# Cross-attention and a mixture of experts on one core: block products over halves of whole experts, and TensorE turning the rows of the first two experts

## The chip, the cores and the metric

The kernel runs on one core of a Trainium2 chip. The metric is the device time of one execution in microseconds (us); the times shown are the median of three runs. The core's engines work side by side, each through its own queue in order: TensorE (PE) multiplies matrices, VectorE (DVE) and ScalarE (ACT) work on elements, GpSimd (POOL) issues the indirect DMAs, and SyncE (SP) issues the plain DMAs. They wait for each other on semaphores.

## The reference

There are 2048 tokens (16 batches of 128) of 512 features. A cross-attention with 32 query heads and 8 key heads of 16 features is added to them; then a feed-forward layer of experts is added:

```python
x = x + xattn(layernorm(x), ctx, ctx)
h = layernorm(x).reshape(-1, 512)
tidx, tw = gate(h)                      # 8 of 32 experts for each token
g = einsum('td,eid->tei', h, w1)        # 512 -> 256 for each expert
u = einsum('td,eid->tei', h, w3)
a = silu(g) * u
routed = einsum('tei,edi,te->td', a, w2, comb)   # comb holds tw at tidx, else 0
out = x + routed + (silu(h @ sw1.T) * (h @ sw3.T)) @ sw2.T
```

All of it is in f32. Only the experts that the gate chose for a token count, so an expert has 2048 x 8 / 32 = 512 tokens on average.

## The kernel before

Attention, the shared expert and the gate come first. What the change touches is the stage of the 32 experts, from about 213 us to the end. The kernel sorts the tokens by expert into 138 slices of 128 slots. The experts stand in a fixed order of places (`ORDER`), each with a fixed capacity (`CAPS`, a multiple of 32) and a room for its tokens (`ROOM`, 440 to 704). A slice that lies on the border of two experts holds rows of both. `begins[k]` is the first slot of place k.

**Rows.** GpSimd gathers each slice's rows by an indirect DMA into one of eight buffers (`gather`, L1432). The rows must be turned, so that the features stand on partitions. For the first slices TensorE does it (`turn`, L1456: sixteen small transposes for two slices, which ScalarE copies out of PSUM, L1473). For all others VectorE transposes blocks of 32x32 inside the slice (`transpose`, L1515, into `blocks`), and ScalarE, with some help from VectorE, copies quarters of 32 tokens into place (`block_copies`, L1512): four copies for each quarter, one for each group of 32 features. Copies for slices that lie next to each other are merged into one. `weigh` (L1524) picks each slot's weight; only then may the buffer be gathered into again.

**Pieces.** The rows of an expert are cut into pieces of at most 512, in buffers `xnT` (four of them) with the results of the up products in `acts` (four). An expert with a capacity over 512, and the first and the last, has two pieces, cut at a multiple of 128 slots; others have one. For an expert of 660 rows the pieces have 384 and 276.

**Up products.** For the first and the last expert they are plain (`direct`, `up`, L1546). For the other thirty they are done by seven block products instead of eight (`seven`, L1615): w1 and w3 (256x512 each, both handled at once in one PSUM bank, the columns of w1 in its first half and those of w3 in its second) are cut into 2x2 blocks, and so are the rows, along the features and along the tokens. VectorE forms sums of weight blocks once per expert (`weight_sums`, L1579: s1, s2, s3, s4, of which s3 overwrites a weight block), sums of token blocks once per piece (`token_sums`, L1610: t1 to t4), and adds the products up (L1643). Each product is four matmuls of 128x128 weights by half a piece's columns. The first product is copied out of PSUM by ScalarE (L1657) before the fifth adds to the same bank; a bank is used twice for three of the four banks of a piece. Silu is ScalarE's (L1651), its product with the other half VectorE's (L1652).

**Down products.** `down` (L1723) multiplies 128 slots by w2 of their expert or experts, two matmuls of 512 columns; ScalarE scales the result by the slots' weights (L1739), and GpSimd adds the rows into the output in HBM (`send`, L1695). Sends of one expert wait for those of the expert before.

**Order.** The order of the work is written out by hand. The loop at the end goes over the pieces, seven steps each (four for `direct`). At each step it issues one product on TensorE, then what became due by it (`soon`, `tick`), then a share of the side work for VectorE and ScalarE (`on_DVE`, `on_ACT`: sums of weights and tokens for the next piece, transposes three pieces ahead, copies two pieces ahead), spread evenly over the steps, then down products of the piece before as planned. One finished slice is always held back (`KEPT`). Weights are loaded three experts ahead, w1 and w3 after an expert's last product, w2 after its last down product (`load_weights`, L1088).

Of the kernel before, what the change touches and what calls it, by code (L numbers as in the profile page):

```python
# [18 lines left out]
P = 128  # L19
# [27 lines left out]
def tile_xattn_moe(  # L47
# [38 lines left out]
    xs = [xpool.tile([P, D], F32, tag=f"x{b}", name=f"x{b}") for b in range(B)]  # L86
    xnT = [
        xtp.tile([P, ND, TB], F32, tag=f"xnT{k}", name=f"xnT{k}") for k in range(NTB)
# [59 lines left out]
    fp = ctx.enter_context(tc.tile_pool(name="fp", bufs=2))  # L148
# [102 lines left out]
    acts = [sap.tile([P, NI, TB], F32, name=f"sa{k}") for k in range(NTB)]  # L251
# [774 lines left out]
    def experts(ups, in_order, later, products):  # L1026
# [384 lines left out]
        for k in range(E):  # L1411
            first, end = begins[k], begins[k + 1]
            if end - first > TB or k in (0, E - 1):
                middle = (first + end + P) // 2 // P * P
                pieces += [(k, first, middle), (k, middle, end)]
            else:
                pieces.append((k, first, end))

        def parts(j):

            for n, (k, first, end) in enumerate(pieces):
                a, b = max(first, j * P), min(end, (j + 1) * P)
                if a < b:
                    yield n, a - j * P, b - j * P, a - first

# [42 lines left out]
        def turned(j, tr, copy):  # L1468
            for n, a, b, col in parts(j):
                for h in range(2):  # L1470
                    a0, b0 = max(a, h * H), min(b, (h + 1) * H)
                    if a0 < b0:
                        copy(  # L1473
                            xnT[n % NTB][:, :, col + a0 - a : col + b0 - a],
# [6 lines left out]
        def block_copies(js):  # L1481
# [3 lines left out]
            for q in range(4):  # L1485
                for j in js:
                    for n, a, b, col in parts(j):
                        if a <= q * Q < b:
                            r, to = j % NB_BUF, col - a
                            last = runs[-1] if runs else None  # L1490
                            if (
                                last
                                and last[0] == q
                                and last[1] == n
                                and last[2] + last[4] == r
                                and last[3] + last[4] * P == to
                            ):
                                last[4] += 1
                            else:
                                runs.append([q, n, r, to, 1])  # L1500
            for q, n, r, to, many in runs:
                for c in range(4):
                    of = blocks[q * Q : (q + 1) * Q, r : r + many, :]
                    of = of.rearrange("p s (k c j) -> p s k c j", c=4, j=Q)[:, :, :, c, :]
                    dst = xnT[n % NTB][c * Q : (c + 1) * Q]
                    at = min(max(to, 0), TB - many * P)
                    dst = dst[:, :, at : at + many * P]
                    dst = dst.rearrange("p k (s t) -> p s k t", t=P)
                    dst = dst[:, :, :, to + q * Q - at : to + (q + 1) * Q - at]
# [8 lines left out]
        def weigh(j):  # L1518
            t = xg.pop(j)
            weighed.add(j)  # L1520
            ks = [pieces[n][0] for n, *_ in parts(j)]
# [17 lines left out]
        def up(n, i, w, banks):  # L1539

            k, first, end = pieces[n]
            m = min(end, begins[k] + ROOM[ORDER[k]]) - first

            acc = banks[w] = ps_p.tile([P, TB], F32, tag="p", name="gu")
            for d in range(ND):
# [3 lines left out]
                    rhs=xnT[n % NTB][:, d, 0:m],  # L1549
# [7 lines left out]
            else:  # L1557
# [3 lines left out]
                        acts[n % NTB][:, i, 0:m], sl[:, 0:m], acc[:, 0:m], ALU.mult  # L1561
# [26 lines left out]
        def width(n):  # L1588
            k, first, end = pieces[n]
            return min(end, begins[k] + ROOM[ORDER[k]]) - first  # L1590

        def halves_of(n):
            h = width(n) // 2
            t = xnT[n % NTB]
            return [t[:, d : d + 2, c * h : (c + 1) * h] for d in (0, 2) for c in range(2)]
# [3 lines left out]
        def token_sums(n):  # L1599


            h = width(n) // 2
            b11, b12, b21, b22 = halves_of(n)
            t1, t2, t4 = (
                late.tile([P, 2, M], F32, tag=name, name=name)[:, :, 0:h]
                for name in ("t1", "t2", "t4")
            )
            tsums[n] = t1, t2, b12, t4
# [3 lines left out]
        def product(acc, w, x, h, first=True):  # L1612
            for i in range(2):
                for d in range(2):
# [5 lines left out]
                        stop=(i == d == 1),  # L1620
# [3 lines left out]
        def seven(n):  # L1624


            k = pieces[n][0]
            h = width(n) // 2
# [4 lines left out]
            b11, _, b21, b22 = halves_of(n)  # L1633
            t1, t2, t3, t4 = tsums.pop(n)

            def bank():
                return ps_p.tile([P, 2, M], F32, tag="p", name="p")

            def kept(name, bufs=2):
                return late.tile([P, 2, M], F32, tag=name, name=name, bufs=bufs)[:, :, 0:h]  # L1640

            def add(out_, a, b):
                soon(lambda: nc.vector.tensor_tensor(out_, a, b, ALU.add))  # L1643

            def gated(of, to, after):
                sl = late.tile([P, 2, M], F32, tag="sg", name="sg", bufs=3)
                if len(of.shape) == 4:
                    sl, g, u = sl[:, :, 0:h], of[:, :, 0], of[:, :, 1]
                else:
                    sl, g, u = sl[:, 0, 0:h], of[:, 0], of[:, 1]  # L1650
                soon(lambda: nc.scalar.activation(sl, g, AF.Silu), after)  # L1651
                soon(lambda: nc.vector.tensor_tensor(to, sl, u, ALU.mult), after + 1)  # L1652

            act = acts[n % NTB]
# [143 lines left out]
        for n in range(len(pieces)):  # L1798
# [41 lines left out]
            for step, _ in enumerate(seven(n) if fast(k) else direct(n)):  # L1840
                tick()
                done += dues[step]
                if step == 1 and by_PE:
                    turn(by_PE)
# [104 lines left out]
```

## Time and profile before

| | us |
|---|---|
| median of three runs | 896.81 (896.02 to 899.05) |
| the profiled execution | 894.69 |
| its span | 892.9 |
| TensorE busy | 872.7 |
| ScalarE busy | 640.9 |
| VectorE busy | 639.3 |
| GpSimd busy | 505.4 |
| first rows of experts turned on TensorE (L1456) | 213.5 |
| last matmul | ends near 883.4 |

Busy times are those of instructions on the engine; those of matmuls overlap, so that two of them can be busy at once. "Idle" times name what ended them. PE stands for TensorE's matmuls, PEld for its weight loads, which run beside matmuls; each f32 matmul of the program shows as two records of each. The granted clock is TensorE's, as a share of full speed.

### The profile page before, as it was taken

What the parts mean: (1) busy time and instruction counts of PE and PEld (TensorE: products, weight loads), DVE (VectorE), ACT (ScalarE), POOL (GpSimd) and SP (SyncE); (2) the same over time, 40 slices, a digit from 0 to 9 for tenths busy, and PEclk for the clock granted to TensorE, in tenths of its full rate; (3) what the DMA queues carried; (4) which work ended last, traced back from release to release, by engine and by line L of the source; (5) the groups of instructions that cost most, each with busy time, mean ns of one, the idle gap of its engine ahead of it and who ended that gap; (6) DMA issues with size and microseconds to landing.
All of it is one profiled execution on the core that took longest, in us unless ns stands there. A gap on an engine that the chain in (4) does not pass through costs nothing.

```text
span 892.9 us, 15745 instructions
## 1 busy us (share of the span) xinstructions
PE 872.7 (98%) x5055; PEld 608.4 (68%) x5055; DVE 639.3 (72%) x1739; ACT 640.9 (72%) x1338; POOL 505.4 (57%) x622
## 2 busy tenths in 40 slices
PE   9999999998999999999999999999999999999995
PEld 5344444544777877878787878787877777777773
DVE  7877778884778776767786777777897767776510
ACT  5888722331989868777888887888897777787441
POOL 4486652674556546556565665666666665543444
PEclk9999999999999999999999999999999999999998
DMA  9111113416578786778787878787877887666534
GB/s 320 40 48 49 48 48 114 145 62 213 161 146 196 159 205 156 175 161 197 175 201 174 208 175 188 179 181 182 203 189 184 195 224 192 156 135 163 81 66 55
DMA packets 59884, 137.28 MB, mean 154 GB/s; under 512 B 12168, under 2 KB 16392, under 8 KB 59792
## 3 DMA queue, kind: packets, MB, share of 16 engines
q0 software_dynamic: 32032, 69.25, 40.4%
q1 hardware_dynamic: 27680, 66.81, 21.9%
q8 instruction: 42, 0.69, 0.4%
q14 instruction: 50, 0.41, 0.2%
q10 hardware_dynamic: 80, 0.13, 0.1%
HBM read 96.71 MB, written 46.73 MB: 161 GB/s over the span
## 4 chain that ended last, share of the span: by engine, by line
PE 93%; issue 2%; POOL 1%; ACT 1%; DVE 1%; DMA 1%; POOLq 0%; ACTq 0%; DVEq 0%
PE p L1615 44%; PE y L1723 25%; PE gu L260 6%; PE sc L465 5%; PE oT L481 3%; PE y L1348 3%; PE x L435 2%; PE gu L1546 2%; POOL out_dram L1695 1%; PE tok L1012 1%; DMA out_dram<-yw,token 1%; PE warm L331 1%; PE lgT L542 0%; PE lg L557 0%; ACT p L475 0%
## 5 line engine op out<-in xcount | busy, mean ns | idle before, releaser
L1695 POOL DMA_INDIRECT out_dram<-yw,token x150 | 244.3, 1629 | 223.6 <-ACT yw L1739 157.5
L1512 ACT COPY xnT<-blocks 32x256 f32<-32x256 f32 (+3 forms) x843 | 358.6, 425 | 11.8
L1723 PE MATMUL y<-wdn,sa 128*128 128x512 f32 (+2 forms) x672 | 259.5, 594 | 0.0
L1615 PE MATMUL p<-xnT,wup 128*128 128x192 f32 (+26 forms) x1152 | 189.6, 311 | 1.2 <-ACT p L1657 1.2
L1615 PEld LDWEIGHTS p<-xnT,wup 128*128 128x128 f32 x1152 | 170.3, 191 | 24.3 <-issue 16.2
L1432 POOL DMA_INDIRECT xgs<-rows,token x138 | 146.8, 1063 | 70.3 <-issue 25.4
L1739 ACT ACTIVATE yw<-y,wt 128x512 f32<-128x512 f32 x138 | 94.8, 687 | 105.5 <-PE y L1723 61.4
L1723 PEld LDWEIGHTS y<-wdn,sa 128*128 128x128 f32 (+2 forms) x672 | 96.1, 171 | 72.8 <-issue 70.0
L1615 PEld LDWEIGHTS p<-t,s 128*128 128x128 f32 x768 | 116.6, 191 | 25.3 <-issue 22.7
L1615 PE MATMUL p<-t,s 128*128 128x128 f32 (+26 forms) x768 | 126.5, 310 | 0.0
L1515 DVE STREAM_TRANSPOSE blocks<-xgs 128x512 f32<-128x512 f32 x134 | 94.8, 707 | 2.9 <-DMA out_dram<-x 2.4
L1643 DVE TENSOR_TENSOR z<-u,p 128x256 f32<-128x256 f32 (+26 forms) x96 | 48.6, 506 | 41.7 <-PE p L1615 38.0
L1615 PEld LDWEIGHTS p<-t,wup 128*128 128x128 f32 x384 | 59.4, 190 | 19.4 <-issue 14.4
L475 ACT ACTIVATE p<-sc 128x1024 f32<-128x1024 f32 x64 | 62.1, 1024 | 13.5 <-PE sc L465 13.5
L1643 DVE TENSOR_TENSOR u<-u,p 128x256 f32<-128x256 f32 (+26 forms) x48 | 24.4, 509 | 58.0 <-PE p L1615 53.3
L1615 PE MATMUL p<-xnT,s 128*128 128x128 f32 (+26 forms) x384 | 64.3, 310 | 0.0
L1615 PE MATMUL p<-t,wup 128*128 128x128 f32 (+26 forms) x384 | 64.0, 310 | 0.0
L1615 PEld LDWEIGHTS p<-xnT,s 128*128 128x128 f32 x384 | 57.2, 191 | 6.1 <-issue 4.5
L260 PE MATMUL gu<-xnT,sup 128*128 128x512 f32 x128 | 59.0, 601 | 0.7 <-ACT ssl L268 0.7
L1006 POOL TENSOR_SCALAR hq<-slice_q,sq 128x138 f16<-128x138 f16 x32 | 35.2, 1113 | 36.3 <-DVE sq L1314 20.1
L1610 DVE TENSOR_TENSOR t<-xnT,t 128x256 f32<-128x256 f32 (+26 forms) x96 | 48.9, 510 | 0.9
L465 PE MATMUL sc<-qT,kz 32*128 32x512 f32 x256 | 44.2, 639 | 0.5 <-DVE qT L456 0.2
(216 smaller groups left out, 1007.4 us busy)
## 6 DMA issues: line engine op xcount, KB each, us to landing
wup<-in_w_dram SPq DMA_DIRECT2D x64, 512.0 KB
wdn<-in_w_dram SPq DMA_DIRECT2D x32, 512.0 KB
rows<-xn SPq DMA_DIRECT2D x16, 256.0 KB
out_dram<-x SPq DMA_DIRECT2D x16, 256.0 KB
x<-in_x_dram SPq DMA_DIRECT2D x15, 256.0 KB
out_dram<-yw,token POOLq DMA_INDIRECT x150
xgs<-rows,token POOLq DMA_INDIRECT x138
cTs<-in_cT_dram SPq DMA_DIRECT2D x4, 256.0 KB
```

The lines of the kernel that those rows point to most:

```text
L260: nc.tensor.matmul(acc, lhsT=sup[:, w, d, ts(i, P)], rhs=xnT[k][:, d, :], start=(d == 0), stop=(d == ND - 1),)
L465: nc.tensor.matmul(scs[j // 2][:, j % 2], lhsT=kzs[b // 4 % 2][rows, b % 4, i, :], rhs=qT[rows], start=True, stop=True, tile_position=(j * ...
L475: nc.scalar.activation(p, sc, AF.Exp, scale=1.0 / HD**0.5)
L1432: nc.gpsimd.indirect_dma_start(out=t, out_offset=None, in_=rows[:, :], in_offset=bass.IndirectOffsetOnAxis(ap=token[:, j : j + 1], axis=0) ...
L1512: yield on_ACT, 1 + many, lambda dst=dst, of=of, copy=copy: copy(dst, of)
L1515: nc.vector.transpose(blocks[:, j % NB_BUF, :], xgs[:, j % NG_BUF, 0:D])
L1610: yield lambda o=out_, a=a, b=b: nc.vector.tensor_tensor(o, a, b, ALU.subtract)
L1615: nc.tensor.matmul(acc[:, i, 0:h], lhsT=w[:, i, d, :], rhs=x[:, d, :], start=(first and i == d == 0), stop=(i == d == 1), skip_group_check ...
L1643: soon(lambda: nc.vector.tensor_tensor(out_, a, b, ALU.add))
L1695: ins = nc.gpsimd.indirect_dma_start(out=flat, out_offset=bass.IndirectOffsetOnAxis(ap=token2[:, k - 1 : k] if a else token[0:b, j : j + 1 ...
L1723: nc.tensor.matmul(y[c0:c1, :], lhsT=acts[n % NTB][:, i, col : col + c1 - c0], rhs=wdn[pieces[n][0] % NW][:, i, :], start=(i == 0), stop=( ...
L1739: nc.scalar.activation(yws[j], y, AF.Copy, scale=wt[:, j : j + 1])
```

## The change

- Every expert now has two pieces. Those of the thirty experts with block products are cut at half the room (`ROOM[ORDER[k]] // 2`), wherever that falls in a slice, and the halves are the token blocks of the seven products: there is one set of seven products for the whole expert.
- An expert with room for up to 512 rows does w1 and w3 together in a bank as before (`both`). A larger one has more columns than half a bank: it does the seven products for w1, then the seven for w3, each of two matmuls per product, in banks of their own. Silu then stands in `act` itself until the w3 pass multiplies it.
- Buffers: one tile `xall` holds the old `xnT` and five half buffers (`half`, 384 columns), another the results of three whole experts (`acts_of`). `blocks` has nine slices and not ten; two finished slices are held back and not one.
- Copies out of the blocks follow the pieces: where a piece begins or ends inside a quarter of 32 tokens, only the tokens of that piece are copied, by a copy of their own. Transposes are now four (half) pieces ahead, copies three.
- TensorE turns all slices of the first two experts (ten), two at a time after each step of the first expert's two pieces; before, it turned four.
- Sums of the next expert's weights are formed in the first half of an expert, sums of its tokens in the second. Down products of the expert before are spread over both halves.

The core of the diff:

```diff
+    HM = max(CAPS) // 2
+    HW = 3 * P
+    NH = 5
+    NA = 3
+    aall = sap.tile([P, NA * NI * 2 * HM], F32, name="sa")
...
+    half = [
+        xall[:, r * ND * HW : (r + 1) * ND * HW].rearrange("p (d t) -> p d t", d=ND)
+        for r in range(NH)
+    ]
...
-            if end - first > TB or k in (0, E - 1):
+            middle = first + ROOM[ORDER[k]] // 2
+            if k in (0, E - 1):
                 middle = (first + end + P) // 2 // P * P
-                pieces += [(k, first, middle), (k, middle, end)]
-            else:
-                pieces.append((k, first, end))
+            pieces += [(k, first, middle), (k, middle, end)]
...
+                    lo, hi = max(a, q * Q), min(b, (q + 1) * Q)
+                    if lo >= hi:
+                        continue
+                    r, to = j % NB_BUF, col + lo - a
+                    last = runs[-1] if runs and runs[-1][0] == q else None
+                    if (
+                        hi - lo == Q
+                        and last
+                        and last[4] == Q
+                        and last[1] + last[5] == r
+                        and last[3] + last[5] * P == to
+                    ):
+                        last[5] += 1
+                    else:
+                        runs.append([q, r, lo - q * Q, to, hi - lo, 1])
...
-        def product(acc, w, x, h, first=True):
-            for i in range(2):
+        def product(acc, w, x, first=True):
+            h = x.shape[-1]
+            outs = range(w.shape[1])
+            for i in outs:
                 for d in range(2):
                     nc.tensor.matmul(
                         acc[:, i, 0:h],
                         lhsT=w[:, i, d, :],
                         rhs=x[:, d, :],
...
-        def seven(n):
+        def seven(k):
+            h = ROOM[ORDER[k]] // 2
+            act = acts_of[k % NA]
...
+            both = 2 * h <= TB
+            size = M if both else HM
...
+            for w in (slice(0, 2),) if both else (slice(0, 1), slice(1, 2)):
+                many = w.stop - w.start
...
+                pa, p1 = bank(), new("p1", many, size, 1)
+                product(pa, a11[:, w], b11)
+                soon(lambda p1=p1, pa=pa: nc.scalar.copy(p1, pa))
+                yield
...
+                product(pa, a12[:, w], b21, first=False)
+                if both:
+                    sl = new("sg", 1, TB, 3)[:, 0]
+                    silu(sl, pa[:, 0], 1)
+                    times(act0, sl, pa[:, 1], 2)
+                elif w.start == 0:
+                    silu(act0, pa[:, 0], 1)
+                else:
+                    times(act0, act0, pa[:, 0], 1)
+                yield
...
-        NB_BUF = 10
-        KEPT = 1
+        NB_BUF = 9
+        by_PE = last_slice(3)
+        KEPT = 2
...
+            if fast(k):
+                if not odd:
+                    of_k = seven(k)
+                steps = 7 if ROOM[ORDER[k]] > TB else 3 if odd else 4
+            else:
+                of_k = direct(n)
+                steps = 4
...
+            if not odd and fast(k + 1):
                 on_DVE += [(4, f) for f in weight_sums(k + 1)]
...
+            to_turn = last_slice(min(n + 4, last_piece)) if n else 0
+            turning = [(5, lambda j=j: transpose(j)) for j in range(n_turned, to_turn)]
...
+            while n_copied <= min(n + 3, last_piece):
+                copying += block_copies(n_copied)
+                n_copied += 1
...
+            if odd and fast(k + 1):
+                on_DVE += [(4, f) for f in token_sums(k + 1)]
+            on_DVE += turning
...
+                if n < 2 and n_turned < by_PE:
+                    turn_next(2)
```

## The prediction

> **What bounds the kernel now.** I read the page's busy times and chain first, then the busy time of every engine in stretches of the expert stage, then TensorE in order of time, and last ScalarE's groups with shapes kept apart. In the page, TensorE is busy 98% of the span, and the chain that ended last is nearly all TensorE; its two largest lines are the block products (L1615) and the down products (L1723).
>
> ```profile
> PE 872.7 (98%) x5055; PEld 608.4 (68%) x5055; DVE 639.3 (72%) x1739; ACT 640.9 (72%) x1338; POOL 505.4 (57%) x622
> PE p L1615 44%; PE y L1723 25%; PE gu L260 6%; PE sc L465 5%; PE oT L481 3%; PE y L1348 3%; PE x L435 2%; PE gu L1546 2%; POOL out_dram L1695 1%; PE tok L1012 1%; DMA out_dram<-yw,token 1%; PE warm L331 1%; PE lgT L542 0%; PE lg L557 0%; ACT p L475 0%
> ```
>
> The stretches (start:end, span, then busy us and instructions of PE, PE's weight loads, DVE, ACT, POOL, then clock, DMA share, GB/s) show TensorE without a gap at full clock. Look at ACT: 87% at its fullest, 84% over the stretch with the experts above 512 rows (245 to 685), 73% over the smaller ones (685 to 850), and in none of them does PE wait.
>
> ```profile
> 400.00:500.00 100.00, 100.00 (x631) 79.42 (x631) 75.17 (x215) 87.18 (x222) 60.35 (x45) 1.00 0.80 184
> 245.00:685.00 440.00, 440.00 (x2579) 345.75 (x2579) 337.71 (x930) 370.75 (x862) 265.52 (x196) 1.00 0.79 183
> 685.00:850.00 165.00, 165.00 (x678) 122.04 (x677) 113.12 (x259) 120.22 (x253) 84.29 (x59) 1.00 0.69 158
> ```
>
> TensorE in order of time. Starts matter here, since busy times of pipelined matmuls overlap: the distance from one start to the next, over the count, is what one matmul costs. Each f32 matmul of the program is two records.
>
> ```profile
> 223.65 0.71 PE L1456 MATMUL trx<-ident,xgs 64*128 64x64 f32 x16
> 224.29 8.90 PE L1546 MATMUL gu<-xnT,wup 128*128 128x256 f32 x40
> ...
> 242.09 1.46 PE L1615 MATMUL p<-xnT,wup 128*128 128x192 f32 x8
> 244.80 1.57 PE L1615 MATMUL p<-xnT,wup 128*128 128x192 f32 x8 [1.24 <-ACT p L1657]
> ...
> 274.50 1.05 PE L1615 MATMUL p<-xnT,wup 128*128 128x120 f32 x8
> 275.39 1.06 PE L1615 MATMUL p<-t,s 128*128 128x120 f32 x8
> 276.28 1.89 PE L1723 MATMUL y<-wdn,sa 128*128 128x512 f32 x4
> ...
> 286.24 1.47 PE L1615 MATMUL p<-xnT,wup 128*128 128x192 f32 x8
> 287.55 1.46 PE L1615 MATMUL p<-t,s 128*128 128x192 f32 x8
> 288.85 1.88 PE L1723 MATMUL y<-wdn,sa 128*128 128x512 f32 x4
> 290.56 1.46 PE L1615 MATMUL p<-t,s 128*128 128x192 f32 x8
> ```
>
> From these: 192 columns cost 1.305/8 = 163 ns, 512 columns 1.71/4 = 428 ns (430 as a median over the stage), 120 columns 0.89/8 = 111 ns. Rows not shown give 190 ns at 224, 203 at 240, 216 at 256, 123 at 144, and 111 at every width from 116 to 128. So a record costs about 2.3 ns + 0.835 ns per column, with a floor of 111 ns that is reached near 130 columns. One wait on another engine is left in the expert stage: 1.24 us at 243.6, for the copy of the first product out of PSUM.
>
> ScalarE's copies out of the transposed blocks, by shape (L1512), and the eviction of a down product:
>
> ```profile
> L1512 ACT COPY xnT<-blocks 32x256 f32<-32x256 f32 x432 | 173.4, 401 | 6.1
> L1739 ACT ACTIVATE yw<-y,wt 128x512 f32<-128x512 f32 x138 | 94.8, 687 | 105.5 <-PE y L1723 61.4 <-issue 33.8 <-ACT sg L1651 4.2
> L1512 ACT COPY xnT<-blocks 32x384 f32<-32x384 f32 x152 | 77.2, 508 | 2.1
> L1512 ACT COPY xnT<-blocks 32x512 f32<-32x512 f32 x99 | 60.8, 615 | 1.3
> L1512 ACT COPY xnT<-blocks 32x128 f32<-32x128 f32 x160 | 47.2, 295 | 2.2
> ```
>
> They fit 188 ns + 0.835 ns per element of a partition, so many small copies are dear.
>
> [...] here 2.2 us of idle before 218.3 were enough for a granted clock of 0.50 from 219 to 222. [...]
>
> **The change on TensorE.** Thirty of the 32 experts use block products. Eighteen have room for more than 512 rows: before, each is two pieces of 28 matmuls, 56 records each, with half widths that add up to half the room (192 + 138 for 660); after, 28 matmuls of the full half width (330). The columns are the same, so 18 x 56 records' fixed part is saved: 1008 x 2.3 ns = 2.3 us. Sixteen of the 36 old pieces are also on the floor: two of 116, two of 120, one each of 122 and 124, two of 126, eight of 128. Against the line these lose 11.8, 8.5, 6.8, 5.2, 3.5 and 1.8 ns a record, in sum 74 ns x 56 = 4.1 us. All new widths lie between 224 and 352, above the floor. Widths of 257 to 352 are not in the trace; 256 costs 0.844 and 512 0.840 ns per column, so between them the error is under 1 ns a record, 1 us in all. Saved: 6.4 us. The twelve smaller experts issue the same matmuls. The down products keep their number and forms, since old piece borders inside an expert lay on multiples of 128 rows.
>
> TensorE now turns ten slices and not four: 6 x 8 = 48 transposes more, at 0.64/16 = 40 ns: +1.9 us. They stand between groups of four matmuls just after the slow stretch of the clock; at half clock they would cost 3.8 us[...]. I take 1.9.
>
> The 1.24 us wait: before, ScalarE runs 31 block copies between 225 and 241 (14.6 us together), and the first product's copy stands behind six more. After, 13 more copies from PSUM (0.28 to 0.38 us) take their place, and block copies begin with the third expert's rows. The wait goes; next in line is the same copy at a later expert, which has some 4.5 us in a large expert (three steps of 1 us and a down product of 1.7) and 6 in a small one before the bank's second product needs it. Saved: 1.2 us.
>
> **The change on the other engines.** ScalarE: the halves begin at any even row, so quarters of slices are cut. 843 copies become 1080: 635 of 256 elements (254.6 us), 80 of 384 (40.6), 199 of 128 (58.7), and 166 of 8 to 120 elements, which no row shows; by the line about 0.25 us (40.7 in all), between the fixed 0.188 (31) and the 0.295 of 128 elements (49). Sum 394.6 against 358.6: +36. Silus fall from 144 to 90, at about 0.19 us of fixed cost: -10. Copies from PSUM after turning: +5. In all +30 us, and it is not even: for experts 1 to 19 the copies go from 599 (248 us) to 681 (258 us), which the silus pay for; for experts 20 to 29 from 196 (90 us) to 366 (125 us). So the first stretch stays at about 84%, and the second goes from 73% to 73 + 34.5/184 = 92%. TensorE's work hides this as long as ScalarE's lag stays below those 4.5 to 6 us. If the cover is gone, every further microsecond is one of the span.
>
> VectorE: 72 token sums and 54 gating products fewer, with the same elements, at 0.145 us of fixed cost: -18; copies 125 to 172: +4; six transposes fewer: -4. Its stages come down to about 0.85 of TensorE's time per expert at most. All of it hidden.
>
> SyncE: each weight load of the up products still stands after the last product of its expert, and w2's after the expert's last down product. One more down product is held back (KEPT 2), so w2's load leaves one down product later; it is needed an expert on. Sums of weights now start in the first half of the expert before and not the last piece: the lead of a load shrinks from about 30 to about 20 us for large experts, which is what the small ones live with now. GpSimd has the same 150 scatters and 138 gathers; those from the eleventh on wait for a weighing that is now earlier (the queue stood idle for 7.6 us before 226.6). The tail is the same: the last four matmul groups and the last three down products end the order in both.
>
> **The sum.** -6.4 + 1.9 - 1.2 = -5.7 us. For ScalarE at 92% I add 1 us of new waits (from 0 to 5): about -4.8. On the profiled execution (894.7 us, 892.9 of it span) that gives 889.9; that execution lies 2.1 us below the median of 896.8, and against the median it gives 892.0.
>
> **The rivals.** First, no change that can be measured: a copy of the first product that comes late in the experts 20 to 29. In ten experts of about 18.4 us, ScalarE has 1.4 us to spare in each; if a quarter of a microsecond is lost at each of the 20 halves, 5 us go and the time is 896. For it: a copy run begins with the slice that VectorE turned last, and there are now two runs where there was one. Against: experts whose ScalarE work came to 1.00 to 1.08 of TensorE's already exist, by the same durations (the ones with room for 560, 544, 540 and 520), and PE waited in none.
>
> Second, slower: ScalarE becomes the bound in those ten experts. It decides once its work and its own waits for VectorE pass 18.4 us per expert, that is once it waits over 0.7 us at each half. At 1.2 us a half, 20 halves cost 10 us: 892 + 10 = 902. Against: a late ScalarE doesn't wait, so the wait shrinks as the lag grows.
>
> Third, more is gained: the cut copies cost no more than 0.19 us, nothing waits, and the earlier gathers smooth the start: 888 to 890. That the products aren't merged is not a case: the instruction order shows 28 per expert.
>
> **How the numbers follow.** The forecast, with its own range of 888.5 to 894.5 (the third case within it), has 0.72; no change 0.15; slower 0.13. The least difference that can be told apart is 0.3%, or 2.7 us: below 894.1 is faster, above 899.5 slower. From the tails of the cases: faster 0.73, same 0.15, slower 0.12. The range is 887.5 to 898.5: the slower case and a little of each side is left out.
>
> **What would show it.** Block products of 260 to 352 columns should follow 2.3 + 0.835 ns per column, and 330 columns start every 278 ns. ScalarE's copies should sum to about 395 us. PE should stay at 100% in each stretch from 300 to 880 of the after trace; PE idle put down to ScalarE's copy of the first product or to evictions in the last quarter would mean the first or second rival. A clock below 1.00 after 224 would make the transposes dearer. The prediction is wrong if a record of 300 columns costs over 260 ns, or PE shows idle above 3 us in the last quarter.

## The result, and the profile after

The changed kernel took 893.68 us in the median of 12 runs (888.46 to 895.18), the kernel before 896.63 in 12 runs beside it (895.11 to 899.19): a ratio of 0.9953, 95% interval 0.9934 to 0.9971. The prediction was 892.0, which is 0.9946 of 896.81. Three more groups of runs, each with its own runs of the kernel before, gave other sizes of the same sign, and this spread turned out to be the main thing to explain (fastest against fastest, the four groups lie closer together: 6.4 to 8.0 us):

| group | before, median us | changed, median us | changed, lowest to highest | ratio, 95% interval |
|---|---|---|---|---|
| first comparison | 896.63 | 893.68 | 888.46 to 895.18 | 0.9953 (0.9934 to 0.9971) |
| e1 to e4 | 894.59 | 885.01 | 883.81 to 887.72 | 0.9897 (0.9876 to 0.9917) |
| e5 to e8 | 895.72 | 890.32 | 887.30 to 893.18 | 0.9937 (0.9914 to 0.9960) |
| e9 to e12 | 897.37 | 891.02 | 887.94 to 893.18 | 0.9938 (0.9918 to 0.9959) |

The profiled execution of the first comparison lies at the upper end of its group: 894.74 us, 893.0 of it span, against 894.69 and 892.9 of the profile before, which is below all 12 runs of the kernel before. So this pair of traces shows no gain at all, and is good for showing where one can get lost. First the page of the changed kernel: busy times and the chain of work that ended last.

```profile
PE 869.7 (97%) x4095; PEld 543.5 (61%) x4095; DVE 629.4 (70%) x1654; ACT 672.3 (75%) x1534; POOL 514.8 (58%) x622
PE p L1651 41%; PE y L1788 24%; PE gu L278 6%; PE sc L483 5%; PE oT L499 3%; PE y L1366 3%; PE x L453 2%; PE gu L1580 2%; POOL out_dram L1760 2%; DMA out_dram<-yw,token 1%; ACT xall L1545 1%; PE tok L1030 1%; PE warm L349 1%; PE lgT L560 0%; PE lg L575 0%
...
L1545 ACT COPY xall<-blocks 32x256 f32<-32x256 f32 (+10 forms) x1080 | 395.6, 366 | 14.3
```

TensorE has 960 records fewer and is still the bound. The chain has a new member, ScalarE's block copies (L1545) with 1%. These copies are 1080 with 395.6 us, as estimated (394.6).

The same execution in stretches (start:end, span, then busy us and instructions of PE, PE's weight loads, DVE, ACT and POOL, then granted clock, DMA share, GB/s):

```profile
218.00:245.00 27.00, 25.12 (x146) 19.28 (x147) 14.31 (x46) 11.63 (x38) 13.19 (x13) 0.87 0.62 182
245.00:300.00 55.00, 52.10 (x172) 30.85 (x171) 40.06 (x100) 50.85 (x133) 28.36 (x23) 1.00 0.66 148
300.00:400.00 100.00, 100.00 (x352) 63.88 (x351) 75.72 (x185) 88.88 (x213) 63.04 (x45) 1.00 0.79 184
...
700.00:800.00 100.00, 100.00 (x392) 74.10 (x391) 77.56 (x192) 92.39 (x251) 61.73 (x44) 1.00 0.83 188
```

From 300 on PE is at 100%, also where ScalarE is at 92% (700 to 800): neither of the first two rivals is to be seen. What is lost is lost between 218 and 300: a granted clock of 0.87 in the mean, and 1.9 and 2.9 us of idle PE. In order of time, PE there (start, us, then the instructions, in brackets the idle time before them and who ended it):

```profile
213.50 0.71 PE L1484 MATMUL trx<-ident,xgs 64*128 64x64 f32 x16
214.14 1.98 PE L1366 MATMUL y<-sdn,sa 128*128 128x512 f32 x4
219.88 3.78 PE L1580 MATMUL gu<-xall,wup 128*128 128x256 f32 x8 [3.75 <-ACT xall L1501]
...
232.79 7.17 PE L1580 MATMUL gu<-xall,wup 128*128 128x256 f32 x32
239.81 1.35 PE L1651 MATMUL p<-xall,wup 128*128 128x352 f32 x4
240.99 2.53 PE L1651 MATMUL p<-t,s 128*128 128x352 f32 x8
243.36 1.35 PE L1651 MATMUL p<-xall,wup 128*128 128x352 f32 x4
244.54 1.88 PE L1788 MATMUL y<-wdn,sa 128*128 128x512 f32 x4
248.07 1.45 PE L1651 MATMUL p<-xall,wup 128*128 128x352 f32 x4 [1.65 <-ACT p L1700]
...
251.84 1.45 PE L1651 MATMUL p<-t,wup 128*128 128x352 f32 x4 [0.73 <-DVE z L1661]
```

Four records of 352 columns take 1.18 us from start to start, 295 ns each, where the line gave 296. But PE waits 3.75 us for the rows of the first expert (2.21 before), and in the second expert 1.65 us for the copy of a first product, the very wait that I had said would go. The clock is at half from 218.8 to 225.6 us; such a stretch is called a slow window below. ScalarE at the same time:

```profile
234.48 1.20 ACT L1501 COPY xall<-trx 128x256 f32<-128x256 f32 x4 [2.21 <-remote]
239.57 0.39 ACT L1590 ACTIVATE sg<-gu 128x256 f32<-128x256 f32 x1 [3.90 <-PE gu L1580]
239.85 3.19 ACT L1545 COPY xall<-blocks 32x256 f32<-32x256 f32 x8
242.95 0.37 ACT L1590 ACTIVATE sg<-gu 128x256 f32<-128x256 f32 x1
243.34 4.20 ACT L1545 COPY xall<-blocks 32x128 f32<-32x128 f32 x13
247.56 0.45 ACT L1700 COPY p<-p 128x352 f32<-128x352 f32 x1
```

Before the copy of the product (L1700) stand 21 block copies of the third expert and two silus, and ahead of these ScalarE stood idle for 3.90 us, waiting for gate and up products that PE had started at 232.79. The silu at 239.57 needs only the first eight of those 32 records, and starts 6.8 us after they began; e5 below has 2.5 us in the same place.

### The profile page after: what moved, and what is told of

Its sections match the earlier page's. It is cut to its first block, busy times and chain, and to the rows that moved or that the text cites. A ratio compares the mean times of both kernels' runs of the same rounds, so it can differ in the third digit from the quotient of the medians.

```text
span 893.0 us, 13862 instructions
## 1 busy us (share of the span) xinstructions
PE 869.7 (97%) x4095; PEld 543.5 (61%) x4095; DVE 629.4 (70%) x1654; ACT 672.3 (75%) x1534; POOL 514.8 (58%) x622
## 4 chain that ended last, share of the span: by engine, by line
PE 90%; issue 3%; ACT 2%; POOL 2%; DVE 1%; DMA 1%; another core or an unknown queue 0%; POOLq 0%; ACTq 0%; DVEq 0%
PE p L1651 41%; PE y L1788 24%; PE gu L278 6%; PE sc L483 5%; PE oT L499 3%; PE y L1366 3%; PE x L453 2%; PE gu L1580 2%; POOL out_dram L1760 2%; DMA out_dram<-yw,token 1%; ACT xall L1545 1%; PE tok L1030 1%; PE warm L349 1%; PE lgT L560 0%; PE lg L575 0%
## 5 line engine op out<-in xcount | busy, mean ns | idle before, releaser
L1545 ACT COPY xall<-blocks 32x256 f32<-32x256 f32 (+10 forms) x1080 | 395.6, 366 | 14.3
L1651 PE MATMUL p<-xall,wup 128*128 128x270 f32 (+27 forms) x720 | 185.6, 394 | 1.6 <-ACT p L1700 1.6
L1651 PEld LDWEIGHTS p<-xall,wup 128*128 128x128 f32 x720 | 136.5, 190 | 46.3 <-issue 16.1
L1651 PE MATMUL p<-t,s 128*128 128x270 f32 (+27 forms) x480 | 125.6, 394 | 0.0
L1661 DVE TENSOR_TENSOR z<-u,p 128x270 f32<-128x270 f32 (+27 forms) x96 | 48.9, 509 | 68.2 <-PE p L1651 62.2
L493 ACT ACTIVATE p<-sc 128x1024 f32<-128x1024 f32 x64 | 62.1, 1024 | 13.8 <-PE sc L483 13.8
L1651 PE MATMUL p<-t,wup 128*128 128x270 f32 (+27 forms) x240 | 63.8, 396 | 0.7 <-DVE z L1661 0.7
L1651 PE MATMUL p<-xall,s 128*128 128x270 f32 (+27 forms) x240 | 63.6, 396 | 0.5 <-DVE z L1661 0.4
L278 PE MATMUL gu<-xall,sup 128*128 128x512 f32 x128 | 59.0, 601 | 0.7 <-ACT ssl L286 0.7
L1651 PEld LDWEIGHTS p<-xall,s 128*128 128x128 f32 x240 | 45.2, 190 | 16.9 <-issue 3.9
L1545 DVE COPY xall<-blocks 32x256 f32<-32x256 f32 (+11 forms) x172 | 45.4, 289 | 3.2
```

The source lines that it names most:

```text
L278: nc.tensor.matmul(acc, lhsT=sup[:, w, d, ts(i, P)], rhs=xnT[k][:, d, :], start=(d == 0), stop=(d == ND - 1),)
L493: nc.scalar.activation(p, sc, AF.Exp, scale=1.0 / HD**0.5)
L1545: yield on_ACT, 1 + many, lambda dst=dst, of=of, copy=copy: copy(dst, of)
L1651: nc.tensor.matmul(acc[:, i, 0:h], lhsT=w[:, i, d, :], rhs=x[:, d, :], start=(first and i == d == 0), stop=(i == outs[-1] and d == 1), ski ...
```

## The experiments

Three groups were run (e1 to e4, e5 to e8, e9 to e12), each on one chip, each with the changed kernel in it. The theory after the first profile: the stage of the block products gains what was predicted or a bit more, and a varying part of it is lost in the start of the expert stage (213 to 263 us). The rivals: the transposes on TensorE are what costs; ScalarE's load takes the gain in the last third; the merged products bring less than the sum said.

**e1, the changed kernel again** (no edit).

> The changed kernel as it is, as the measure for the others of this group. If its gain is that of the profile compared so far (steady stage about 5 us shorter, start of the expert stage 3 us later), its ratio to the kernel before is again 0.995 to 0.997. Start theory (two windows of half clock at 218.8 to 225.6 us cost about 3 us): its single times fall with the mean granted clock, about 1.7 us for each window, so 0.990 should be some 5 us longer than 0.997. Rival (the transposes themselves or ScalarE's load eat the gain): times do not follow the clock.

Measured: 885.01 us, ratio 0.9897 (0.9876 to 0.9917), 8.7 us less than the same kernel took in the first comparison. PE in the profile of e1, from the first transposes to the first products of the third expert:

```profile
216.51 0.71 PE L1484 MATMUL trx<-ident,xgs 64*128 64x64 f32 x16
217.15 1.98 PE L1366 MATMUL y<-sdn,sa 128*128 128x512 f32 x4
218.97 1.89 PE L1580 MATMUL gu<-xall,wup 128*128 128x256 f32 x8
...
236.70 1.35 PE L1651 MATMUL p<-xall,wup 128*128 128x352 f32 x4
...
256.70 1.11 PE L1651 MATMUL p<-xall,wup 128*128 128x280 f32 x4
```

There is no idle ahead of the gate and up products and none in the second expert, which takes 20.0 us and not 23.3. The transposes were reached 3.0 us later than in the first profile (two slow clock windows at 118.5 to 125.3 us, not at 218), and yet the first block product came 3.1 us earlier. ScalarE began to copy the transposed rows 0.74 us after the transposes began (217.25); in the first profile it was 4.0 us (217.52 after 213.50). The times do follow the clock: 883.8 to 884.4 us at a mean of 0.996 to 0.997, 887.7 at 0.993. That the windows stand at 218 was wrong for this execution.

**e2 and e3, the idle time filled**, in the changed kernel and in the one before (nine matmuls there):

```
         shared_down(last_down)
+        filler = (ps_y, ps_z)[(last_down + 1) % 2].tile([P, D], F32, tag="y", name="filler")
+        for _ in range(14):
+            nc.tensor.matmul(filler[:, 0:P], lhsT=wz, rhs=wz, start=True, stop=True)
```

> Fourteen matmuls of zeros (222 ns each, 3.1 us in all, no reader) stand in the 3.75 us in which TensorE is idle ahead of the first gate and up products. Start theory: no idle time, so no window of half clock from 218.8 to 225.6; the first window takes 1.2 us from work (2.3 us of it fall on work) and the second 1.7, so 2 to 3 us less than the changed kernel, a ratio to before near 0.992, and a mean clock of 0.997 or more. Rival, that the completions of the first transposes are seen late whatever the clock: the first gate and up product still starts at 219 to 220 us, and if the windows stay too, the time is that of the changed kernel.

> The kernel before with nine matmuls of zeros (2.0 us) in its own gap of 2.2 us ahead of the first gate and up products. It had one window of half clock, all of it on work: start theory expects 1.7 us less (ratio 0.998), that is less than the filling brings the changed kernel (2 to 3 us). If it gains as much or more, the gap is no loss of the change, but one that both have.

Measured: e2 887.11 us (0.9925, 0.9905 to 0.9945), 2.1 us more than e1; e3 893.42 (0.9992, 0.9979 to 1.0005). On this chip the rows are there in time, so the filling only pushes work back. e3's profile still shows a wait of 2.20 us for the copy of the first product (1.24 in the profile before): the kernel before can't use all of an early start. This fits the larger gain of this group, but no profile of the kernel before without the filling was taken on this chip, so it isn't shown. A gain of 2 to 3 us is refuted here; for the case with idle the group couldn't decide (e10 takes it up).

**e4, without the turning on TensorE**: the changed kernel, but only four slices turned by PE, the other six by VectorE's transposes and ScalarE's block copies in the first expert, as in the kernel before.

```
-        by_PE = last_slice(3)
+        by_PE = last_slice(1)
...
-        n_copied = 4
+        n_copied = 2
...
-            to_turn = last_slice(min(n + 4, last_piece)) if n else 0
+            to_turn = last_slice(min(n + 4, last_piece)) if n else last_slice(3)
```

> The changed kernel with TensorE turning four slices as before, and VectorE and ScalarE the other six (first two experts). My prediction's terms: minus 1.9 us of transposes, plus 1.2 for the wait that comes back: 0.7 us less than the changed kernel. Theory that the turning on TensorE costs more than its transposes (late completions, a late first product copy of 1.65 us with 0.73 us behind it, the second window of slow clock): 3 to 4 us less, ratio to before 0.991 to 0.992. Rival, that the gap before the first product alone is the loss: within 1 us of the changed kernel, with the idle 3.75 us unchanged.

Measured: 898.8 us, ratio 1.0057 (1.0037 to 1.0077), 13.8 us more than e1. All three expectations miss. In its profile, a wait of VectorE and the one of PE that follows:

```profile
241.50 0.89 DVE L1642 TENSOR_TENSOR t<-xall 128x704 f32<-128x704 f32 x1 [5.29 <-ACT xall L1545]
243.38 4.62 PE L1651 MATMUL p<-t,s 128*128 128x352 f32 x8 [8.26 <-DVE t L1642]
```

The second product waits 8.26 us for VectorE's token sums, these wait 5.29 us for ScalarE's block copies, and the clock is at half for 10.24 us from 237.2. Before, the first piece of the second expert needed the rows of one half only; products of whole experts need all its rows, and sums of them, before their second product. So the two parts of the change belong together: the turning on TensorE doesn't save a wait of one microsecond, as my sum has it, but is what lets the merged products start in time. (How VectorE's work is ordered in this variant is mine; a better order might take some of the 8.26 us away.)

**e5, the changed kernel again**, with another chip's group.

> The changed kernel again, as the measure for this group. It was 0.9953 of the kernel before at first and 0.9897 in the group before this one, where TensorE went from the last shared product straight to the first gate and up products (no idle, first block product 17.7 us after them) instead of waiting 3.75 us there and three times more in the second expert. If the signals between engines around 213 to 240 us come late by chance in each execution, this group's ratio lies between the two, and its profile shows one of the two patterns; if it is a matter of the chip, one of the two comes back whole.

Measured: 890.32 us, ratio 0.9937. Its profile is the one to hold against the profile before, since both have one slow clock window at 218 and about the same idle there (2.45 and 2.21 us). PE in the profile before:

```profile
218.31 5.41 PE L1546 MATMUL gu<-xnT,wup 128*128 128x256 f32 x16 [2.21 <-issue]
...
236.47 1.46 PE L1615 MATMUL p<-xnT,wup 128*128 128x192 f32 x8
```

PE in e5, then ScalarE:

```profile
213.49 0.71 PE L1484 MATMUL trx<-ident,xgs 64*128 64x64 f32 x16
214.13 1.98 PE L1366 MATMUL y<-sdn,sa 128*128 128x512 f32 x4
218.56 3.59 PE L1580 MATMUL gu<-xall,wup 128*128 128x256 f32 x8 [2.45 <-issue]
...
230.42 7.17 PE L1580 MATMUL gu<-xall,wup 128*128 128x256 f32 x32
237.43 1.35 PE L1651 MATMUL p<-xall,wup 128*128 128x352 f32 x4
...
242.16 1.88 PE L1788 MATMUL y<-wdn,sa 128*128 128x512 f32 x4
243.88 1.35 PE L1651 MATMUL p<-xall,wup 128*128 128x352 f32 x4
```

```profile
217.31 1.20 ACT L1501 COPY xall<-trx 128x256 f32<-128x256 f32 x4 [13.11 <-PE y L1366]
...
232.91 0.43 ACT L1590 ACTIVATE sg<-gu 128x256 f32<-128x256 f32 x1
233.18 3.19 ACT L1545 COPY xall<-blocks 32x256 f32<-32x256 f32 x8
236.40 0.38 ACT L1590 ACTIVATE sg<-gu 128x256 f32<-128x256 f32 x1
236.81 4.19 ACT L1545 COPY xall<-blocks 32x128 f32<-32x128 f32 x13
241.02 0.45 ACT L1700 COPY p<-p 128x352 f32<-128x352 f32 x1
```

The same 21 block copies stand ahead of the product's copy, which ends at 241.5, and PE needs it at 243.9: 2.4 us of cover. The first profile had used these up and 1.65 more, because ScalarE began these copies 6.7 us later, PE its products only 2.4 us later.

**e6, the turning on TensorE alone**, in the kernel before:

```
-                by_PE = range(n_turned, slices_of(1)[0])
-                n_copied = n_turned = slices_of(1)[0]
+                by_PE = range(n_turned, slices_of(3)[0])
+                n_copied = n_turned = slices_of(3)[0]
...
-                if step == 1 and by_PE:
-                    turn(by_PE)
+                if by_PE:
+                    gather_next()
+                    turn(by_PE[:2])
+                    by_PE = by_PE[2:]
```

> The kernel before with one part of the change alone: TensorE turns ten slices and not four, in pairs after each group of gate and up products. My sum has plus 1.9 us for 48 more transposes and minus 1.2 us for the first product's copy, which was late by 1.24 to 2.2 us: about plus 0.7 us (ratio 1.000 to 1.001). If the turning on TensorE is itself what shortens the start (no wait at the first product, copies early), it is faster by 1 to 2 us (0.998 to 0.999). If transposes at the start are what costs, it is 3 us slower (1.003).

Measured: 895.54 us, ratio 0.9993 (0.9981 to 1.0006): no change, and a cost of 3 us is excluded. Its profile has no wait for the copy of a first product: the block products take 639.89 us from the first of them (240.47) to the last three down products (880.36), where the kernel before took 641.59 (236.47 to 878.06). PE in e6:

```profile
240.47 1.46 PE L1615 MATMUL p<-xnT,wup 128*128 128x192 f32 x8
...
880.36 1.88 PE L1723 MATMUL y<-wdn,sa 128*128 128x512 f32 x4
```

So the old wait costs 1.70 us, of which 1.24 are recorded as idle, and the turning takes about that much on TensorE.

**e7, the third expert's first block copies later**, out of the way of that product's copy:

```
-            while n_copied <= min(n + 3, last_piece):
+            while n != 1 and n_copied <= min(n + 3, last_piece):
```

> The changed kernel with the block copies of the third expert's first half (21 on ScalarE) made in the second expert and no longer ahead of it. If the first product's copy is late because they stand in front of it (1.65 us, with 0.73 and 0.4 us behind it), this saves up to 2.8 us where the wait is seen and nothing where it isn't; the price could be a late third expert, whose token sums need these rows: then a wait of VectorE's sums shows at its first products and the kernel is slower.

Measured: 891.97 us (0.9954, 0.9934 to 0.9973) against 890.32 for e5: not better. The wait moves into the second half of the products of the same expert (0.68 us for ScalarE's copy, 1.05 and 0.19 for VectorE's sums). The reading, which no further run confirms: the copies have to be made by then anyway.

**e8 and e12, more work for ScalarE** in the experts 20 to 29: copies of 128 elements of a zero tile which nothing reads, four in each half (e8) or two (e12).

```
             on_DVE += [(c, f) for a, c, f in copying if not a]
+            if 20 <= k < E - 2:
+                gap = len(on_ACT) // 4
+                for i in range(4):
+                    on_ACT.insert(i * (gap + 1), (2, lambda: nc.scalar.copy(spare, wz)))
```

> The changed kernel with 80 copies more on ScalarE (128 elements, 0.295 us each, four in each half of experts 20 to 29): 2.36 us more per expert of 18.4 us, so its load there goes from 92 or 93% to 105 or 106%. Rival of my prediction, that ScalarE at 92% is at its limit: every microsecond more is one of the time, 20 us and more. My theory, that TensorE hides it until ScalarE's load passes 100%: only what lies above 100% shows, about 1 us in each of ten experts, less what ScalarE may fall behind in the end: 7 to 11 us, nearly all of it after expert 22, in waits of PE for copies of the first product and for evictions.

> The changed kernel with 40 copies more on ScalarE (two in each half of experts 20 to 29, 1.18 us in each expert of 18.4 us): its load there goes from 93% to 99%. Twice as many took its load to 106% and cost 5.7 us in the median, 7.2 us in the profile. If TensorE hides ScalarE's work up to 100% and no further, this costs nothing (below 1 us); if ScalarE at 93% were already at the edge, it costs half of that, 3 us or more.

Measured: e8 896.06 us, ratio 0.9993 (0.9976 to 1.0009) beside 0.9937 of e5, 5.7 us more. From the third expert's first product to the last three down products it takes 621.50 us (258.55 to 880.05), e5 614.29 (257.43 to 871.72): 7.2 us more for 23.6 us of added copies. e12: 892.53 (0.9954, 0.9939 to 0.9970) beside 891.02 of e9. Its profile takes 615.01 us for that stretch, e9's 615.03, so the 1.5 us of the medians didn't come from there. By the count it was to reach 99%; the stretch below has 95.6%. The stretch from 700 to 800 in e5, e12 and e8, one fence each:

```profile
700.00:800.00 100.00, 100.00 (x397) 75.10 (x396) 76.87 (x186) 93.41 (x254) 57.33 (x42) 1.00 0.81 190
```

```profile
700.00:800.00 100.00, 100.00 (x396) 75.02 (x395) 75.65 (x185) 95.58 (x267) 60.57 (x43) 1.00 0.82 188
```

```profile
700.00:800.00 100.00, 98.13 (x386) 72.86 (x385) 70.45 (x173) 96.07 (x271) 58.09 (x41) 1.00 0.76 181
```

ScalarE at 93 and 96% costs PE nothing. Where more is asked of it than time allows (105% by the count), it stays at 96% and PE stops. In e8 PE waits five times for it or behind it between 756 and 815 us; four of these:

```profile
756.47 1.98 PE L1788 MATMUL y<-wdn,sa 128*128 128x512 f32 x4 [1.29 <-ACT yw L1804]
775.58 1.98 PE L1788 MATMUL y<-wdn,sa 128*128 128x512 f32 x4 [0.58 <-ACT yw L1804]
...
811.05 1.86 PE L1651 MATMUL p<-xall,wup 128*128 128x236 f32 x8 [1.42 <-ACT p L1700]
814.67 1.93 PE L1788 MATMUL y<-wdn,sa 128*32 128x512 f32 x16 [1.75 <-ACT yw L1804]
```

It is the eviction of the down products that comes late first, then the copy of the first product. That was the second rival's mechanism; the changed kernel stands some 7% short of it.

**e9, e10 and e11, the idle time again**: the changed kernel, the filling of e2, and a version that turns the first two slices one shared down product earlier:

```
-        *downs, last_down = downs
+        *downs, next_down, last_down = downs
...
         turn_next(last_slice(0))
+        shared_down(next_down)
+        for f in products:
+            f()
+        products.clear()
         shared_down(last_down)
```

> The changed kernel again, as the measure for this group. The three groups so far gave 0.9953, 0.9897 and 0.9937 of the kernel before; if the signals out of the first transposes come 3 to 4 us late on this chip as in the first and third group, TensorE idles 2.2 to 3.8 us ahead of the first gate and up products and the ratio is 0.993 to 0.996; if they come after 0.7 us as in the second group, there is no idle and the ratio is 0.989 to 0.991.

> The changed kernel with the fourteen matmuls of zeros (3.1 us) ahead of the first gate and up products, for the second time. It cost 2.1 us where there was no idle to fill. Where there is idle of 2.2 to 2.5 us: the filling overshoots it by 0.7 us, but the window of half clock from about 218.5 to 222 us, worth 1.7 us of work, should not come: about 1 us less than the changed kernel. If the window comes all the same, 0.7 us more.

> The changed kernel with the first two slices turned one shared down product (1.72 us) earlier, so that two of these and not one stand between the transposes and the first gate and up products. The second slice's rows land at 212.5 us, so the transposes, due at 211.8, wait some 0.8 us. Where the signals come 3 to 4 us late: the idle of 2.2 to 2.5 us falls to about 1.5 us in all, in two parts, and no window of half clock should follow: 2 to 3 us less than the changed kernel. Where they come at once: 0.8 us more. If the window of half clock comes whatever the idle: 0.8 us less in the first case.

Measured: e9 891.02 us (0.9938), e10 888.57 (0.9916, 0.9897 to 0.9934), e11 889.49 (0.9927, 0.9909 to 0.9945). The late signal is there: ScalarE's first copy 3.9 us after the transposes, and PE idle for 2.57 us in e9. PE in e9, then in e11:

```profile
221.26 1.99 PE L1580 MATMUL gu<-xall,wup 128*128 128x256 f32 x8 [2.57 <-issue]
```

```profile
211.81 0.46 PE L1484 MATMUL trx<-ident,xgs 64*128 64x64 f32 x8
212.69 0.47 PE L1484 MATMUL trx<-ident,xgs 64*128 64x64 f32 x8 [0.42 <-DMA xgs<-rows,token]
213.09 3.70 PE L1366 MATMUL y<-sdn,sa 128*128 128x512 f32 x8
217.32 1.99 PE L1580 MATMUL gu<-xall,wup 128*128 128x256 f32 x8 [0.53 <-issue]
```

The idle falls from 2.57 to 0.95 us in two parts, and this execution has no slow window at all; waits of 0.56, 0.73 and 0.38 us on VectorE, up to 276 us, give some of it back. Both versions are faster than e9 in the medians, by 2.5 and 1.5 us, but their intervals overlap its own, and the lowest times are alike (887.86, 888.33, 887.94). e9 had no slow window after its idle time either, so the slow window that e10 and e11 were to avoid wasn't there in its profile. On the chip of e2 the filling cost 2.1 us. So no version was shown to beat the changed kernel; turning earlier is the one that I would follow up, since it puts work and not zeros into the gap.

## Why the prediction was right, point by point

The time and the ratio came out as predicted (892.0 and 0.9946; measured 893.68 and 0.9953, then 0.9897, 0.9937 and 0.9938), and all four medians are faster by more than 0.3%. How near the first ratio came is in part luck: where PE hardly waited at the start (e1), the gain was larger than forecast (0.9897 of 896.81 is 887.6, below the forecast's own 888.5 to 894.5), and in the first comparison a loss that the sum didn't have took some of it back. The terms of the sum, read from e5 against the profile before:

| term of the sum | predicted us | measured us | how |
|---|---|---|---|
| merged products | -6.4 | -7.3 | 634.29 us (e5, 237.43 to 871.72) less 1.72 for one more down product in it, against 639.89 without waits (e6) |
| 48 more transposes | +1.9 | +2.4 | first gate and up to first block product, 18.87 against 18.16, and 1.72 of a down product that left |
| wait for the first product's copy | -1.2 | -1.7 | e6 against before |
| ScalarE in experts 20 to 29 | +1.0 | 0 | no PE idle after 300 us in e5; e8 and e12 |
| start of the first gate and up products | 0 | +0.3 | 218.56 against 218.31 |
| sum | -4.8, as put there | -6.3 | spans 886.5 against 892.9: -6.4 |

- **Merging** held, by its two reasons. The new widths lie on the line or 1 ns under it (295 ns for 352 columns, 235 for 280), and the sum of the measured distances over all 36 old and 18 new widths gives -6.9 us; the last 0.4 us were not traced further. The stretch of 634.29 us is the same to the last digit in e1, e2, e5 and e10, the four profiles without a wait in it.
- **Transposes**: 50 ns each in their place and not 40. The 0.64 us of a group are seen again, so what is added lies in the change from one kind of matmul to the other: between two groups of transposes eight gate and up records take 1.93 us from start to start (e5, 222.72 to 224.65), in a row 1.75 (230.42 to 237.43, by four). e6 agrees that the cost is small.
- **The wait**: the amount was about right where it went, the reason was not. I let the block copies begin with the third expert's rows and didn't count that these stand in front of the first product's copy: 21 of them, 7.4 us, which leave 2.4 us of cover (e5). The wait went in e1, e2, e5, e8, e9 and e10, and came back in the first profile with 1.65 us and in e12 with 0.82. e4 shows what I had missed: the rows of the whole expert are now due at its second product.
- **ScalarE at 92%**: right at its fullest (93% from 700 to 800 in e5), and now with a margin. The copies cost what the line of small copies said (394.8 us in e5, 394.6 estimated), and PE lost nothing up to 96%. The load is spread more evenly than forecast: 87% from 245 to 685 and 88% from 685 to 850 in e5, where I had about 84 and 92.
- **What the sum left out is the start.** The prediction priced dearer transposes at half clock (3.8 us for all 48; in the first profile sixteen took 1.05 us at a clock of 0.50, from 223.59 to 224.64, against 0.64), but didn't take that into its sum, and it had no price for a longer idle or for rows and signals that come late. The start of the expert stage decides what is seen of the gain. The first profile loses 6.5 us to e5 there, all of the gain: 2.4 until the first block product (1.3 of longer idle, the rest a second window at half clock), 3.3 in the second expert (two waits of 1.65 and 0.73 us and what it takes PE to start again), 0.8 in the third (one wait of 0.38 us).

The wait for the first product's copy follows how late ScalarE's third silu starts after the first of its products. It is 2.0 to 3.8 us in e1, e2, e5, e8, e9 and e10, which have no such wait; 5.0 in e11, where PE waits 0.73 us for VectorE instead; 6.0 in e12 and 6.8 in the first profile, which wait 0.82 and 1.65 us. So the loss in the second expert goes with a signal that is late there too, and not with the late start alone.

Why the rows are late in one execution and not in the next is settled only in part. In the four profiles of e1 to e4 ScalarE starts 0.7 us after the first transposes; in all others, of both kernels, 2.4 to 4.0 us, wherever in time these transposes stand. In those traces many of the DMA landings (the records that a transfer has arrived) between 213 and 219 us are missing too (mostly one to nine of 16 are there), while the DMA engines are full (a share of 0.92 to 1.08 from 214 to 218) in these and in those of e1 to e4 alike. Whether that is the chip, the traffic or the recording itself, no run here separates.

The slow windows are settled better. Slow stretches last 3.41, 6.83 or 10.24 us in the traces, that is one, two or three times the same length. In the two traces of the first comparison the clock falls once more near the end, and the distance is again a whole number of that length: from the return to full clock at 222.11 us to the fall at 887.70 it is 665.6 us or 195 times 3.413 (before), from 225.60 to 887.79 it is 662.2 us or 194 times (changed kernel). So I count windows of 3.41 us on from each execution's own slow stretches; that they run on between them is an estimate from these distances. In e5 the window from 215.00 to 218.42 has 2.3 us without work, and the next one is slow. In e9 the idle of 2.57 us falls across the border of two windows (220.2 us, counted from the trace), 1.5 us in one and 1.1 in the other, and no slow window follows. In the first profile of the changed kernel the slow window itself has 1.1 us of idle, and a second slow one follows. So about the same idle (2.2 to 2.6 us) was followed by no slow window or by one, which by my estimate costs some 1.7 us (half of 3.41, at a clock of 0.50), and what differs in these traces is its phase; the first profile's idle of 3.75 us brought two. The other traces fit. With 2.2 us or more of the idle in one window (before, e5, e7, e12) a slow one follows; where a border splits it into 1.71 and 0.78 (e6), 1.53 and 0.93 (e8) or 1.52 and 1.05 (e9), none does. An amount of idle isn't the whole rule: five executions (e1, e6, e8, e9, e10) have two slow windows at 118 us instead, in work that the change doesn't touch, after windows with only 1.2 to 1.5 us of idle. Phase seems to decide there too: in these five a window begins between 114.4 and 115.1 us, in the other nine none does.

## What to carry to other kernels

Merging matmuls off the floor of the narrow ones (111 ns from 116 to 128 columns here) paid what a line of cost against width said, and could be priced from start distances to within a microsecond (6.4 us against 7.3 measured). But a larger unit of work needs all its inputs earlier: look for who has to deliver them at the very first unit, where nothing is prefetched yet, and count the copies that stand in front of the first eviction there. And when one profile shows nothing gained, compare it with a second one before explaining it: here the first pair hid a gain of 6.4 us behind one unlucky start.

## What the runs showed of the hardware

- After an idle stretch of PE of 2.2 to 2.6 us the granted clock fell to 0.50 in three traces, which have the idle within one of the 3.41 us windows as counted above (2.21 us in the profile before, the shortest), and stayed at 1.00 right after it in three, where a border splits it.
- A wait of PE cost more than its recorded idle in the two places compared: 1.70 us for 1.24 (before against e6), and 0.74 for 0.38 (e9 against e5), so some 0.4 us more. Part of it shows in the first records after the wait, which follow each other more slowly (1.48 and 1.41 us for eight, and not 1.31, in the profile before from 244.80).
- ScalarE was 95.6% busy from 700 to 800 us without PE losing anything (e12, PE at 100%), and stayed at 96.1% where it was the bound (e8, PE at 98.1%).
- Signals out of the first transposes reached ScalarE after 0.7 us in one group (e1 to e4) and after 2.4 to 4.0 us in the others, with the same instructions.
